# Three-layer graph convolution on one core: layer 1's edge gathers released by matmul units, weight loads moved, keys in bfloat16

## The chip, the cores and the metric

The kernel runs on one core of one Trainium2 chip. The core has five engines that run their own instruction streams and meet through semaphores: TensorE (PE, with its weight loads shown as PEld), VectorE (DVE), ScalarE (ACT), GpSimd (POOL) and SyncE (SP), which here only issues transfers. The metric is the device time of one execution in microseconds; lower is better.

## What is computed

A node table `x` of 2500 x 256 is normalized by rows and rectified. Then come three edge convolutions over 80,000 edges (`src`, `dst`, sorted by `dst`), and a final product over the input and the three layers' results.

```python
def _edge_conv(x, src, dst, W, b):
    xi = x[dst]
    xj = x[src]
    m = jnp.concatenate([xi, xj - xi], axis=-1) @ W + b
    s = jax.ops.segment_sum(m, dst, num_segments=N)
    cnt = jax.ops.segment_sum(jnp.ones((dst.shape[0],), m.dtype), dst, num_segments=N)
    return s / jnp.maximum(cnt, 1.0)[:, None]
...
h = jnp.maximum(_layernorm(x, axis=-1), 0.0)
xs = [h]
for W, b in ((W0, b0), (W1, b1), (W2, b2)):
    h = jax.nn.relu(_edge_conv(h, src, dst, W, b))
    xs.append(h)
return x + jnp.concatenate(xs, axis=-1) @ Wf + bf
```

Because the message is linear, a layer is `counts @ (h @ Wb)` plus a degree term times `h @ (Wt - Wb)`, where `counts` holds how often each source feeds each destination.

## The kernel before

**Tiling.** The 2500 nodes are padded to 20 tiles of 128 (`NT`). All but 112 of them (`FEW`) are destinations of 398 windows of 6 nodes. The windows form five groups (`NG`) of up to 80 windows, 480 destinations each. For a group the kernel holds `a`, the counts of 128 x 20 x 480. A count block is made of comparisons on VectorE (`compare`: one-hot `one_m`, `one_n` from the keys), small bfloat16 matmuls into a PSUM `bank` (`counts`) and casts by ScalarE (`take_counts`).

**Before layer 1.** The list `order` (line 1040) is written out by hand. Each name is a step: `st`, `rs`, `sq`, `sc` are row statistics, `N` normalizes a pair of tiles, `T` and `R` turn it on TensorE and take it into `hT` on ScalarE, `Z` and `F` are products, `H` and `L` split `Z` into a high part `zh` and a low part `zl`. `pick`, `pk`, `sg`, `se` find where each window's edges begin (`pick_half` on TensorE, `count_half` as a Sign pass on ScalarE, `search` on VectorE), `ge` fetches the edges with GpSimd, and `ka`, `km`, `kb`, `kt`, `k1`, `k2` make the keys: `key_low` and `key_high` write `km` and `kn` in float32, `key_turn` turns them by four transposes into a PSUM bank, `key_copy` spreads them. `warm8` and `warm12` put that many matmuls without use ahead of the next step that takes a bank (`keep_warm`, `warmed`). Every engine keeps the order in which the steps are written, since the calls go through `InOrder`.

**Layer 1.** The loop at line 1079 runs the five groups. `layer` (line 989) yields after each of 24 units: 20 units of four matmuls (two halves of the output, `zh` and `zl`), and four of `hT` by the weights `wt`. Between units the loop places pieces of other work: the building of the next group's counts (`build`), and a chain `extra` of smaller pieces, one piece a unit (up to two in group 0): `degrees(i)` counts the edges of each node with ScalarE passes and small matmuls, `finish` completes `a` and stores it to DRAM by SP for reuse in the later layers (four transfers of 1.2 MB), `later_loads` has SP load layer 2's weights `wb`, `wt`, `wf` and the bias rows `b_all`, `bf_sb`.

**The 112 few nodes.** They are summed edge by edge. `gather(0)` (line 918) issues 56 indirect transfers from GpSimd, each fetching one row of `z_dram` for each of 128 partitions, into the 8 slots of `sums` in turn; from the ninth on they add to the slot. They stand before the loop over the groups, and each waits only for the transfer eight before it. Their source `z_dram` is written by `keep_nodes`: `zh` by SP, `zl` added by GpSimd. After the last group `add_sums(8)` adds the eight slots by halving on VectorE and splits the result into two parts, and `layer_few` multiplies it in on TensorE. Layer 2 begins behind it.

Layers 2 and 3 have the same groups, with counts loaded back from DRAM and the few nodes' rows gathered in pairs (`gather_pairs`), every second gather of which waits for the unit that was issued last.

Of the kernel before, what the change touches and what calls it, by code (L numbers as in the profile page):

```python
# [8 lines left out]
F32 = mybir.dt.float32  # L9
I32 = mybir.dt.int32  # L10
AF = mybir.ActivationFunctionType
OP = mybir.AluOpType
# [256 lines left out]
BF16 = mybir.dt.bfloat16  # L269
# [19 lines left out]
def run(it):  # L289
    for _ in it:  # L290
        pass
# [16 lines left out]
def chain(*its):  # L308
    for it in its:
        yield from it  # L310
# [3 lines left out]
def by_windows(ctx: ExitStack, tc: tile.TileContext, x, src, dst, Ws, bs, Wf, bf, out, missing):  # L314
    nc = tc.nc
    PE, DVE, ACT, POOL, SP = nc.tensor, nc.vector, nc.scalar, nc.gpsimd, nc.sync
    PEo, DVEo, POOLo, ACTo, SPo = (InOrder(tc, e) for e in (PE, DVE, POOL, ACT, SP))
    P = 128
# [11 lines left out]
    CAP = CH * P  # L330
    SKIP = 2
    FEW = 112
    EDGES = 56
    SUMS = 8
# [3 lines left out]
    WG = (NW + P - 1) // P  # L338
# [3 lines left out]
    N1 = NT * (W - SKIP)  # L342
# [32 lines left out]
    def bank():  # L375
        return ps[-1].tile([P, 512], F32, name="bank")
# [16 lines left out]
    ident_b = const.tile([P, P], BF16, name="ident_b")  # L393
# [6 lines left out]
    lim = const.tile([P, WG], F32, name="lim")  # L400
# [3 lines left out]
    sums = const.tile([P, SUMS, D], F32, name="sums")  # L404
# [9 lines left out]
    pw = pre.enter_context(tc.tile_pool(name="prework", bufs=2))  # L414

    shift = pp.tile([P, P + 1], F32, name="shift")
    ident = shift[:, :P]
# [99 lines left out]
    first = pp.tile([P, 1], F32, name="first")  # L517
    after = pp.tile([P, 1], F32, name="after")
    behind = pp.tile([P, WG * P], F32, name="behind")
    pick = pp.tile([P, WG * P], F32R, name="pick")  # L520
# [104 lines left out]
        POOLo.tensor_scalar(who, who, NONE, None, op0=OP.add)  # L625

    def key_low(i):
        km = pw.tile([P, CAP], F32, name="km")
        ACTo.copy(km, parts[i][0])
        parts[i][0] = km  # L630

    def key_high(i):

        es = edges[i][0]
        hi_i = es if i < WG - 1 else pp.tile([P, CAP], I32, name="hi_i")
        DVEo.tensor_scalar(hi_i, es, ~(P - 1), 4, op0=OP.bitwise_and, op1=OP.logical_shift_right)
        kn = pw.tile([P, CAP], F32, name="kn")
        DVEo.scalar_tensor_tensor(kn, away[:, i, :], float(W + 1), hi_i, op0=OP.min, op1=OP.add)
        parts[i].append(kn)

    def key_turn(i):
        pt = bank()
        for q, k in enumerate(parts[i]):
            for j in range(CH):
                PEo.transpose(pt[:, q * CAP + j * P:q * CAP + (j + 1) * P], k[:, j * P:(j + 1) * P], ident)
        parts[i] = pt

    def key_copy(i, q):
# [229 lines left out]
    def finish(g, a):  # L878
        c0, n = group_of(g)
        if n < GS:  # L880
            DVEo.memset(a[:, :, n:].bitcast(F32), 0.0)
        ACTo.copy(a[PAD:PAD + 1, NT - 1, :n], cnt[PAD:PAD + 1, c0:c0 + n])
        if g + 1 < NG:
            store_a(g, a)
        yield
# [18 lines left out]
    def keep_nodes(l, a, b):  # L904
# [10 lines left out]
        for i, q in ways:  # L915
            POOLo.dma_start(to[:, i, q, :], tiles_of(zl)[:, i, q, :], accum_op=OP.add)

    def gather(l):

        for e in range(EDGES):  # L920
            POOLo.indirect_dma_start(
                out=sums[:, e % SUMS, :], out_offset=None, in_=z_dram[l][:, :],
                in_offset=bass.IndirectOffsetOnAxis(ap=who[:, e:e + 1], axis=0),
                **({"compute_op": OP.add} if e >= SUMS else {}))

    def add_sums(n):

        DVEo.scalar_tensor_tensor(sums[:, 0, :], b_all, deg[:, WG - 1, 0:1], sums[:, 0, :], op0=OP.mult, op1=OP.add)
        while n > 1:
            n //= 2  # L930
            DVEo.tensor_add(sums[:, :n, :], sums[:, :n, :], sums[:, n:2 * n, :])
        two = room(F32R)
        DVEo.tensor_copy(two[:, 0, :], sums[:, 0, :])
        DVEo.tensor_sub(two[:, 1, :], sums[:, 0, :], two[:, 0, :].bitcast(F32))
        return two
# [18 lines left out]
    def gather_pairs(l):  # L954

        got = []
        for k in range(EDGES // 2 + PAIRS):
            if k >= PAIRS:
                if k == PAIRS + 1:
                    DVEo.tensor_add(sums[:, :2, :], got[0], got[1])  # L960
                elif k > PAIRS:
                    DVEo.tensor_add(sums[:, :2, :], sums[:, :2, :], got[k - PAIRS])
            if k < EDGES // 2:
                two = room()
                got.append(two)
                for i in range(2):
                    d = POOLo.indirect_dma_start(
                        out=two[:, i, :], out_offset=None, in_=z_dram[l][:, :],
                        in_offset=bass.IndirectOffsetOnAxis(ap=who[:, 2 * k + i:2 * k + i + 1], axis=0))
                    if k >= PAIRS and i == 0:  # L970

                        tc.add_manual_dep(d.ins, unit[0].ins.name, mybir.DependencyInfo(
                            mybir.DependencyClass.Sync, mybir.DependencyReason.DATA), reason="spread over the layer")
            if k >= PAIRS - 1:
                yield

# [10 lines left out]
    unit = [None]  # L987

    def layer(l, g, a, own, PE=PE, ACT=ACT):
# [31 lines left out]
    a = new_a(0)  # L1021
# [16 lines left out]
        "warm": keep_warm,  # L1038
    }
    order = """  # L1040
        long warm8 lim io first next dstr st0 rs0 sq0 sc0 warm12 N0 pick pk00 sg00 pk01 sg01 st1 T0 pk11 R0 st4 rs1 sq1 pk30 se0
        sg11 sc1 Z0 pk20 N1 st5 sg30 ge0 T1 st6 R1 rs3 F0 sg20 pk21 sq3 st7 pk10 H0 F1 rs4 st3 sq4 sc4 G0 st9
        sc3 L0 sg21 N6 pk31 ka0 kb0 Z1 N5 st8 N7 G1 T6 rs5 sg10 sg31 km0 T5 se1 kt0 R6 H1 st2 F6 sq5 sc5 k10 k20
        rs2 Z6 ge1 L1 T7 B0 R5 R7 Z5 B1 C0 B2 ka1 G6 H6 N9 H5 C1 T9 F7 E0 ge2 kb1 R9 sq2 km1 E1 kt1 C2 B3 k21 Z9
        k11 N8 L6 B4 E2 L5 C3 B5 C4 T8 E3 E4 C5 V9 R8 E5 ge3 ka2 H9 sc2 Z7 H7 F8 G7 B6 N3 N2 ka3 km2 T2 R2 km3
# [19 lines left out]
    def later_loads():  # L1065
        load_wb(1, SPo)
        load_wt(1, SPo)
        load_wf(1, SPo)
        load_b_all(0, SPo)
        SPo.dma_start(bf_sb, bass.AP(tensor=bf.tensor, offset=bf.offset, ap=[[0, P], [1, D]]))  # L1070
        yield
# [2 lines left out]

    held = None
    LATE = [NT] * 4
    gather(0)
    extra = chain(degrees(0), finish(0, a), later_loads(), degrees(1))
    for g in range(NG):
        at = {}  # L1080
        own = LATE
        if g + 1 < NG:
            a1 = new_a(g + 1)
            one = build(g + 1, a1)
            left = -(-len([b for b in windows if b[0] == g + 1]) // TURN)
            units = NT + DC * DC
            at = {(i + 1) * (units - 1) // left - 1 for i in range(left)}
            if g:
                own = [u + 1 - i for i, u in enumerate(sorted(at)[1:5])]
        else:  # L1090
            extra = shares()
        for u, _ in enumerate(layer(0, g, a, own, PEo, ACTo)):
            if u in at:
                next(one)
            next(extra, None)
            if g == 0 and u % 2:
                next(extra, None)
            if g == 0 and u == NT // 2 + 3:
                by_count(0)
            if u == NT - 1 and g + 1 < NG:  # L1100
                run(extra)
                by_count(g + 1)
                if g == NG - 2:
                    by_count(NG)
        run(extra)
        if g + 1 < NG:
            run(finish(g + 1, a1))
            held, a = a, a1
        extra = chain(degrees(g + 2) if g + 2 < WG else ())
    layer_few(0, add_sums(SUMS))  # L1110
    DVEo.tensor_sub(ws[1][0], ws[1][0], ws[1][1])
    tiles = {NG - 1: a, NG - 2: held}
# [81 lines left out]
```

## Time and profile before

| | us |
|---|---|
| median of 3 runs | 502.18 (501.98 to 502.33) |
| the profiled execution | 508.13 |
| its span | 506.4 |
| end of the last vector instruction in it | 500.5 |
| start of layer 1's first group | 61.3 |
| start of layer 2's products | 205.3 |

The profile comes from an execution of its own, so its times add up to 508.13 and not to the median. Some stretches and groups to know (columns of the second block: line, engine, operation, out and in, count, busy time and mean, idle time before them):

```profile
DVE  7999987699898932581235141426722231214043
ACT  5676675563734330430000000005200000000000
POOL 3687307888888840005787582600175645451000
DMA  9426998696999991359798999973335889897033
```

Each digit is the busy share, in tenths, of one fortieth of the span (12.7 us). Layer 1 fills the fifth to the sixteenth digit.

```profile
L282 POOL DMA_INDIRECT sums<-z_dram,who x56 | 91.4, 1632 | 23.9 <-issue 16.8
L1004 PE MATMUL pa<-a,zh 128*128 128x480 f32 (+1 forms) x400 | 151.8, 380 | 0.0
L282 PE MATMUL bank<-one_n,one_m 128*128 128x120 bf16 (+1 forms) x796 | 43.2, 209 | 0.6 <-issue 0.4
```

The 56 gathers keep GpSimd busy for 1.63 us each. The main matmuls have a mean of 380 ns but overlap: in the chain of time 80 of them take 17.3 us, 0.217 us each. Instructions that go through `InOrder` all carry line 282, whatever step they come from.

### The profile page before, as it was taken

Reading aid. Unit: us, or ns where it says so; the run is one execution under the profiler, and the core shown is the slowest. Engines: PE = TensorE matmul, PEld = TensorE weight load, DVE = VectorE, ACT = ScalarE, POOL = GpSimd, SP = SyncE. Lnnn points to the kernel's source line nnn. Section 1 sums busy time; section 2 is a strip of 40 time slices with the busy share of each in tenths; the row PEclk is TensorE's granted clock in tenths of the full one; section 3 lists DMA queues with packets and bytes.
Section 4 is the critical chain, followed back from the end, with each engine's and each line's share of the span. In section 5 each row is a group of like instructions: output and inputs, shape, how many; then the busy total and the mean of one; then the engine's idle time right before and its main releaser. Section 6 shows DMA issues by size and latency. Waiting matters only on the chain.

```text
span 506.4 us, 7649 instructions
## 1 busy us (share of the span) xinstructions
PE 493.7 (97%) x2863; PEld 403.8 (80%) x2863; DVE 266.2 (53%) x670; ACT 136.2 (27%) x309; POOL 252.5 (50%) x234
## 2 busy tenths in 40 slices
PE   8999999899999999999999999999999999999994
PEld 4888887578888788888787878878887878788784
DVE  7999987699898932581235141426722231214043
ACT  5676675563734330430000000005200000000000
POOL 3687307888888840005787582600175645451000
PEclk9999999899999999999999999999999999999999
DMA  9426998696999991359798999973335889897033
GB/s 280 145 65 128 240 278 263 150 340 90 364 151 260 231 80 19 115 204 395 279 327 295 270 248 278 85 129 104 115 104 212 347 270 246 255 249 79 2 110 99
DMA packets 42104, 100.01 MB, mean 197 GB/s; under 512 B 5209, under 2 KB 32170, under 8 KB 36394
## 3 DMA queue, kind: packets, MB, share of 16 engines
q1 hardware_dynamic: 22762, 70.06, 37.6%
q0 software_dynamic: 18368, 28.26, 34.4%
q10 hardware_dynamic: 928, 1.11, 0.7%
q8 instruction: 24, 0.39, 0.3%
q14 instruction: 22, 0.18, 0.1%
HBM read 61.79 MB, written 38.26 MB: 198 GB/s over the span
## 4 chain that ended last, share of the span: by engine, by line
PE 91%; DVE 5%; DMA 1%; POOL 1%; issue 1%; ACT 0%; SPq 0%; DVEq 0%; ACTq 0%
PE pa L1004 34%; PE pa L282 22%; PE bank L811 10%; PE bank L282 8%; PE bank L787 7%; PE pa L1009 6%; PE pz L282 3%; DMA acc<-in_x_dram 1%; DVE st L282 1%; DVE one_m L282 1%; DVE one_n L282 1%; POOL acc L282 1%; DVE zl L282 0%; DVE mv L282 0%; DVE away L282 0%
## 5 line engine op out<-in xcount | busy, mean ns | idle before, releaser
L282 POOL DMA_INDIRECT one_m<-z_dram,who x112 | 113.0, 1009 | 151.1 <-DVE acc L282 79.7
L1004 PE MATMUL pa<-a,zh 128*128 128x480 f32 (+1 forms) x400 | 151.8, 380 | 0.0
L1004 PE MATMUL pa<-a,zl 128*128 128x480 f32 (+1 forms) x400 | 151.6, 379 | 0.0
L282 POOL DMA_INDIRECT sums<-z_dram,who x56 | 91.4, 1632 | 23.9 <-issue 16.8
L282 DVE TENSOR_TENSOR sums<-sums,one_m 128x512 f32<-128x512 f32 x52 | 36.0, 692 | 103.3 <-DMA one_m<-z_dram,who 101.2
L1004 PEld LDWEIGHTS pa<-a,zl 128*128 128x128 f32 x400 | 75.0, 187 | 12.0
L1004 PEld LDWEIGHTS pa<-a,zh 128*128 128x128 f32 x400 | 75.1, 188 | 10.4
L282 PE MATMUL pa<-a,zh 128*128 128x480 f32 (+1 forms) x200 | 81.2, 406 | 0.1
L282 DVE TENSOR_TENSOR one_m<-iota_m,key_m 128x1024 bf16<-128x1024 bf16 x100 | 68.8, 688 | 18.5 <-PE bank L282 15.4
L282 PE MATMUL pa<-a,zl 128*128 128x480 f32 (+1 forms) x200 | 75.7, 378 | 0.2 <-issue 0.2
L1012 ACT ACTIVATE hT<-pa 128x960 f32<-128x960 f32 (+1 forms) x10 | 9.7, 966 | 230.5 <-PE pa L1009 208.6
L282 ACT CAST a<-bank 128x480 fp32r<-128x480 f32 x100 | 51.7, 563 | 60.0 <-PE bank L282 52.7
L282 DVE TENSOR_TENSOR one_n<-iota_n,key_n 128x480 bf16<-128x480 bf16 x200 | 63.9, 360 | 0.0
L282 DVE SCALAR_TENSOR_TENSOR acc<-bank,share,acc 128x256 f32<-128x256 f32 x60 | 28.5, 483 | 58.7 <-PE bank L811 58.0
L811 PE MATMUL bank<-wf,hT 128*128 128x256 f32 x240 | 53.7, 379 | 0.5 <-ACT hT L282 0.5
L811 PEld LDWEIGHTS bank<-wf,hT 128*128 128x128 f32 x240 | 45.5, 190 | 9.8 <-issue 3.4
L282 PEld LDWEIGHTS <-one_m 128*128 128x128 bf16 x796 | 37.6, 98 | 10.5 <-issue 5.8
L282 PEld LDWEIGHTS pa<-a,zh 128*128 128x128 f32 x200 | 37.7, 188 | 8.8 <-issue 3.7
L282 PE MATMUL bank<-one_n,one_m 128*128 128x120 bf16 (+1 forms) x796 | 43.2, 209 | 0.6 <-issue 0.4
L282 PEld LDWEIGHTS pa<-a,zl 128*128 128x128 f32 x200 | 37.7, 188 | 6.9 <-issue 2.1
L787 PE MATMUL bank<-wb,hT 128*128 128x256 f32 x160 | 35.0, 380 | 0.0
L1009 PE MATMUL pa<-hT,wt 128*128 128x480 f32 (+1 forms) x80 | 33.8, 564 | 0.1
(148 smaller groups left out, 420.9 us busy)
## 6 DMA issues: line engine op xcount, KB each, us to landing
a<-a_dram SPq DMA_DIRECT2D x24, 1200.0 KB
a_dram<-a SPq DMA_DIRECT2D x20, 1200.0 KB
out_dram<-acc SPq DMA_DIRECT2D x19, 128.0 KB
z_dram<-one_m SPq DMA_DIRECT2D x16, 128.0 KB
z_dram<-sums SPq DMA_DIRECT2D x16, 128.0 KB
acc<-in_x_dram POOLq DMA_DIRECT2D x4, 512.0 KB
z_dram<-zh SPq DMA_DIRECT2D x7, 256.0 KB
z_dram<-zl POOLq DMA_DIRECT2D x7, 256.0 KB
```

Source lines behind the costliest of these rows:

```text
L282: return self.tc.keep_in_program_order(call(*args, **kwargs))
L787: PE.matmul(pz[:, :D], hT[:, c, t * P:(t + 1) * P], ws[l][1][:, c, :], start=(c == 0), stop=(c == DC - 1))
L811: PE.matmul(po[:, :D], hT[:, c, t * P:(t + 1) * P], wfs[l][:, c, :], start=(c == 0), stop=(c == DC - 1))
L1004: unit[0] = PE.matmul(pa[:, o, :n], tile_of(z, i)[:, o * P:(o + 1) * P], a[:, i, :n], start=(i == 0 and z is zh), stop=(z is zl and last[o ...
L1009: unit[0] = PE.matmul(pa[:, o, :n], ws[l][0][:, c, o * P:(o + 1) * P], hT[:, c, c0:c0 + n], start=False, stop=(last[o] == (kind, i, o)))
L1012: ACT.activation(hT[:, :, c0:c0 + n], pa[:, :, :n], AF.Relu)
```

## The change

Six edits stand in the diff:

- `km` and `kn` are bfloat16, and `key_turn` transposes them with the bfloat16 identity into a bank seen as bfloat16.
- In `order`, `N0 T0` come before `pick`, `R0` right after `pk00`, `Z0` before `pk11`; `warm12` becomes `warm8` and so stands ahead of `T0`.
- `gather` is a generator. The loop over the units takes a gather from it when enough units have passed: gather k from unit 10 + 1.4 k on for the first twelve, then one for every 1.2 units. Each gather gets a wait on the last matmul of the unit issued last (`behind_unit`).
- `later_loads` leaves the chain of group 0, where an empty step takes its place, and becomes the chain of group 3.
- `add_sums(8)` adds slots 4 to 6 to slots 0 to 2, then slots 1 to 3 to slot 0 one by one, and slot 7 last.
- `degrees` stays where it was.

```diff
     def key_low(i):
-        km = pw.tile([P, CAP], F32, name="km")
+        km = pw.tile([P, CAP], BF16, name="km")
...
-        kn = pw.tile([P, CAP], F32, name="kn")
+        kn = pw.tile([P, CAP], BF16, name="kn")
...
     def key_turn(i):
-        pt = bank()
+        pt = bank().bitcast(BF16)
         for q, k in enumerate(parts[i]):
             for j in range(CH):
-                PEo.transpose(pt[:, q * CAP + j * P:q * CAP + (j + 1) * P], k[:, j * P:(j + 1) * P], ident)
+                PEo.transpose(pt[:, q * CAP + j * P:q * CAP + (j + 1) * P], k[:, j * P:(j + 1) * P], ident_b)
         parts[i] = pt
...
+    def behind_unit(d):
+
+        tc.add_manual_dep(d.ins, unit[0].ins.name, mybir.DependencyInfo(
+            mybir.DependencyClass.Sync, mybir.DependencyReason.DATA), reason="spread over the layer")
+
     def gather(l):
 
         for e in range(EDGES):
-            POOLo.indirect_dma_start(
+            behind_unit(POOLo.indirect_dma_start(
                 out=sums[:, e % SUMS, :], out_offset=None, in_=z_dram[l][:, :],
                 in_offset=bass.IndirectOffsetOnAxis(ap=who[:, e:e + 1], axis=0),
-                **({"compute_op": OP.add} if e >= SUMS else {}))
+                **({"compute_op": OP.add} if e >= SUMS else {})))
+            yield
 
     def add_sums(n):
 
         DVEo.scalar_tensor_tensor(sums[:, 0, :], b_all, deg[:, WG - 1, 0:1], sums[:, 0, :], op0=OP.mult, op1=OP.add)
-        while n > 1:
-            n //= 2
-            DVEo.tensor_add(sums[:, :n, :], sums[:, :n, :], sums[:, n:2 * n, :])
+
+        if n > 2:
+            DVEo.tensor_add(sums[:, :3, :], sums[:, :3, :], sums[:, 4:7, :])
+            for i in (1, 2, 3):
+                DVEo.tensor_add(sums[:, 0, :], sums[:, 0, :], sums[:, i, :])
+        DVEo.tensor_add(sums[:, 0, :], sums[:, 0, :], sums[:, n - 1, :])
         two = room(F32R)
...
                     if k >= PAIRS and i == 0:
-
-                        tc.add_manual_dep(d.ins, unit[0].ins.name, mybir.DependencyInfo(
-                            mybir.DependencyClass.Sync, mybir.DependencyReason.DATA), reason="spread over the layer")
+                        behind_unit(d)
...
-        long warm8 lim io first next dstr st0 rs0 sq0 sc0 warm12 N0 pick pk00 sg00 pk01 sg01 st1 T0 pk11 R0 st4 rs1 sq1 pk30 se0
-        sg11 sc1 Z0 pk20 N1 st5 sg30 ge0 T1 st6 R1 rs3 F0 sg20 pk21 sq3 st7 pk10 H0 F1 rs4 st3 sq4 sc4 G0 st9
+        long warm8 lim io first next dstr st0 rs0 sq0 sc0 warm8 N0 T0 pick pk00 R0 sg00 pk01 sg01 st1 Z0 pk11 st4 rs1 sq1 pk30 se0
+        sg11 sc1 pk20 N1 st5 sg30 ge0 T1 st6 R1 rs3 F0 sg20 pk21 sq3 st7 pk10 H0 F1 rs4 st3 sq4 sc4 G0 st9
...
-    gather(0)
-    extra = chain(degrees(0), finish(0, a), later_loads(), degrees(1))
+    FIRST, SLOW = 10, 12
+    edge = gather(0)
+    fetched, passed = 0, 0
+    extra = chain(degrees(0), finish(0, a), [None], degrees(1))
...
         for u, _ in enumerate(layer(0, g, a, own, PEo, ACTo)):
+
+            passed += 1
+            while fetched < EDGES and passed >= FIRST + 1.4 * min(fetched, SLOW) + 1.2 * max(fetched - SLOW, 0):
+                next(edge)
+                fetched += 1
...
-        extra = chain(degrees(g + 2) if g + 2 < WG else ())
+        extra = chain(degrees(g + 2) if g + 2 < WG else later_loads() if g + 2 == WG else ())
     layer_few(0, add_sums(SUMS))
```

On the engines this gives: TensorE's transposes of the keys become pairs of a weight load and a matmul, GpSimd's instructions keep their order, SP has the five loads behind the twelve stores of groups 1 to 3 instead of ahead of them, and VectorE has one instruction more.

## The prediction

> **What bounds the kernel now.** I read the page first (busy shares, the chain that ended last), then the chain in order of time, then stretches of one layer-1 group each, then single engines where a stretch was too long.
>
> ```profile
> span 506.4 us, 7649 instructions
> PE 493.7 (97%) x2863; PEld 403.8 (80%) x2863; DVE 266.2 (53%) x670; ACT 136.2 (27%) x309; POOL 252.5 (50%) x234
> PE 91%; DVE 5%; DMA 1%; POOL 1%; issue 1%; ACT 0%; SPq 0%; DVEq 0%; ACTq 0%
> ```
>
> TensorE carries the time. In the chain by time VectorE leads from 8.65 to 34.75 us, GpSimd's normalizing takes 3.5 us, and from 38.30 us TensorE is on the chain almost without a break. Only work that TensorE does after 38.3 us, what starts it there, and gaps in it count. The gaps lie in one place, the end of group 0 of layer 1. Stretches of one group each (columns: busy time of PE, PEld, DVE, ACT, POOL, then granted clock, DMA share, GB/s):
>
> ```profile
> 61.30:84.45 23.15, 23.15 (x211) 19.63 (x209) 18.73 (x49) 15.80 (x46) 7.73 (x7) 1.00 0.93 278
> 84.45:91.14 6.69, 4.03 (x41) 2.57 (x41) 3.82 (x11) 2.75 (x8) 5.47 (x4) 1.00 0.58 155
> 91.14:97.21 6.07, 5.94 (x28) 2.73 (x26) 5.16 (x14) 2.84 (x7) 4.90 (x4) 0.72 0.46 65
> 97.21:125.48 28.27, 28.27 (x257) 22.98 (x258) 24.22 (x63) 15.67 (x39) 24.31 (x14) 1.00 0.88 241
> 125.48:154.09 28.61, 28.61 (x257) 23.05 (x256) 25.22 (x66) 16.20 (x41) 24.34 (x15) 1.00 1.00 235
> ```
>
> Groups 1 and 2 take 28.3 and 28.6 us; group 0 takes 35.9 (61.30 to 97.21). The chain there, and ScalarE just before:
>
> ```profile
> 84.61 0.73 PE bank L282 x16
> 85.34 0.11 issue
> ...
> 86.12 0.41 issue
> ...
> 88.97 0.48 issue
> ...
> 91.33 4.07 PE pa L282 x6
> ```
>
> ```profile
> 82.90 0.56 ACT L282 CAST a<-bank 128x480 fp32r<-128x480 f32 x1 [1.17 <-PE bank L282]
> 84.38 0.56 ACT L282 CAST a<-bank 128x480 fp32r<-128x480 f32 x1 [0.93 <-remote]
> 85.84 0.56 ACT L282 CAST a<-bank 128x480 fp32r<-128x480 f32 x1 [0.90 <-PE bank L282]
> ```
>
> "issue" means that TensorE waited for nothing the profile shows. Its count matmuls (bank) ended at 81.9 us, but the three casts that take them start 1.48 and 1.46 us apart, and TensorE's own instructions then come in clumps 0.7 us apart until 90.84. After that the clock is halved: six pa matmuls take 4.07 us. What the stretch should cost: 24 bank (1.07 us, as on the row at 100.05), 4 pa of 0.217, 12 degree matmuls (0.68, twice the part of six in the 1.41 row), 8 of hT by wt (3.22, the L1009 rows) and 16 bank (0.72): 6.56 us. It took 12.76. The stall is worth **6.2 us**.
>
> **What the Trainium skill says.** "TensorE: Matmul & The Clock Gate", Part 1, "What's actually happening": an idle window of about 3.4 us puts the array at half clock, a busy one restores it. The trace agrees: between 84.45 and 91.14 PE is busy 4.03 of 6.69 us, and the granted clock is 0.50 in 93 to 95 us. "Runtime: NRT & Kernel Launch", "Instruction fetch mechanics": instructions come over a DMA queue of their own in 16 KiB blocks. The trace has that queue (24 packets, 0.39 MB), one packet of it in 84 to 85 us, yet the clumps go on for five microseconds after it, so I do not rest the cause on it. The same page, "The ~15µs preamble/postamble breakdown", names a gap of about 6.2 us between a profile's total and the time of an execution without one. Here 508.13 - 502.18 = 5.95 us. I take this for the usual gap, that is, the stall is in the timed runs too; no run here shows it, and it is the largest doubt below.
>
> **The change part by part.**
>
> *Weights later.* Five loads leave SP's place at 76.03 to 79.99 us and go behind the stores of group 3, the last at about 157 us. In 76 to 85 us queue 1 moved 2.24 MB; 1.2 MB of that is a last store, 1.0 MB the loads, the last two of them 128 KB each in rows of 1 KB. They are the only thing in this stretch that no other group has: gathers run beside stores at 98 to 110 us, and alone at 112 to 125, with TensorE full. So I take the loads, in their mix with the first gathers, for the cause and credit the whole -6.2 us. Lower bound 0, if they are innocent or do the same at the new place; upper bound 6.5. What waits for them: wb at the L787 matmuls (205 us), b_all at the sums (185 us); landing near 170 us they are in time. SP carries nothing else between.
>
> *Gathers held back.* Gather k is released at unit 10 + 1.4k for the first twelve, then every 1.2 units. A unit is 28.4/24 = 1.19 us, in group 0 about 1.22 without the stall. Gather 0: unit 10 ends at 74.1 us, but it starts only at 76.36 anyway, behind the last zl add. Gather 5: unit 17, 82.1 us against 83.44 now; gather 9: unit 23, 89.5 against 89.54; gather 12: unit 27, 94.3 against 95.31. From there a release each 1.43 us meets a GpSimd that needs 1.54 + 0.30 = 1.85. So without the stall nothing moves by more than a microsecond. Behind the waiting gather GpSimd has only gathers. The wait itself: the layer-2 gathers with a TensorE wait already met show the same 0.30 us gap as those without. Cost 0; bound 0.03 us x 44 = 1.3 us at the end.
>
> *Last slot last.* Now:
>
> ```profile
> 182.96 1.54 POOL L282 DMA_INDIRECT sums<-z_dram,who  x1 [0.30 <-issue]
> 192.02 2.41 DVE L282 TENSOR_TENSOR sums<-sums 128x1024 f32<-128x1024 f32 x3 [5.98 <-DMA sums<-z_dram,who]
> 204.40 0.41 PE L282 MATMUL pa<-only,one_m 128*128 128x112 f32 x2
> ```
>
> The last gather lands at 192.0; adds (2.41) and split (0.72) end at 195.2; TensorE takes the result at 204.40: 9.2 us of cover. After the change one add (0.43) and the split follow the landing, 1.2 us. But the moved loads take 3.7 us of all DMA engines (queue 1 held 78.9% of them for the 9 us of 76 to 85, 7.1 us; a store of 1.2 MB at the 0.35 MB per us of group 3's stores is 3.4 of it), now inside 157 to 192 us, where the engines are full (share 1.00). The last landing goes to at most 195.7, the result is ready at 196.9, and TensorE, 6.2 us earlier, wants it at 198.2. Cover 1.3 us, cost 0; bound +2.4 if the landing slips by twice the loads' time.
>
> *bfloat16 keys.* Sixteen transposes. Four in float32 take 0.44 us (39.39 to 39.83); bf16 count matmuls of 100 columns on average take 1.07/24 = 0.045, so 128 columns 0.057 and four 0.23. Two of the four turns lie after 38.3 us: -0.42. The other two are behind VectorE: 0. The vector and scalar instructions that write the keys keep their number and shape: 0, bound -0.1 each.
>
> *First tiles ahead of the picks.* Eight warming matmuls instead of twelve, then TensorE turns tile pair 0 before the two pick matmuls; ScalarE takes hT (0.59) before the Sign passes; product Z0 (1.6 us) goes before pk11, pk30, pk20. Turn 0 can run at about 7.9 us (normalized at 7.81), the passes shift by 0.2. But pk11 waits behind Z0 until 10.8, its Sign pass slips from 10.67 to 11.2, and ScalarE's following normalizing and roots with it: VectorE's reciprocal at 15.18, which already waits 0.2 us for a root, comes 0.4 later, and VectorE's chain to 38.3 has no slack. +0.4; bounds 0 (ScalarE catches up in its 0.35 us pauses) and +0.8.
>
> *Degrees*: an empty step keeps their places: 0.
>
> Sum: -6.2 - 0.42 + 0.4 = -6.2. The profiled execution 508.13 becomes 501.9; less 5.95, the runs shown **496.0**.
>
> **The rivals.**
>
> *A, forecast, chance 0.47*: 496.0, own range 494.8 to 498.2 (early part -0.8, late sums +2.2).
>
> *B, nothing comes of it, 0.26*: the stall is only in profiled executions, stays with the gathers alone, or reappears near 165 us where the loads now mix with accumulating gathers. For it: the clumps last to 90.84, three microseconds after the last loads' packets, with gathers still going; and the 5.95 us gap is as large as the stall. Against: b_all's single load at 186 us beside gathers stalls nothing. What is left is -0.42 + 0.4: 502.2, from 501.2 to 503.2.
>
> *C, slower, 0.27*: the late sums become the bound at the end of layer 1. The place: layer_few's matmuls, with all of layer 2 queued behind them on TensorE. If the timed runs hold no stall, the cover is these 1.3 us and the landing slips by up to 7.4 us (loads in 1 KB rows taking turns with 1 KB gathers): 199.4 + 1.2 - 198.2 = +2.4 us, 504.6. It decides once the last landing passes 197.0 us (203.2 if the stall stays). For it: DMA share 1.00 from 125 to 184 us, a landing already 7.5 us behind the last issue. Against: with the stall gone the same slip only trims the gain.
>
> **How the numbers follow.** What this kernel's timing can tell from no change is about 0.2%, 1.0 us. Faster: A and 0.03 of B; same: 0.22 of B; slower: C with the rest of B, 0.28. The range, 494.8 to 504.0, holds A, B and a good part of C.
>
> **What would show it.** Right: in the new profile group 0 ends near 90.7 us, the clock stays at 1.00 in all of layer 1, no "issue" on the chain there; the five loads land near 165 to 170 us; the last gather lands by 196 and VectorE's sums never hold TensorE; the product chain starts within 0.5 us of 38.3. Wrong: clumps 0.7 us apart anywhere in 76 to 185 us, or a TensorE wait on VectorE's split before L787. If the profile loses 6 us and the timed runs do not, B's first reading holds.

## The result and the profile after

The changed kernel is slower: 505.39 us median of 8 executions (503.57 to 507.76), against 502.24 us (501.98 to 502.59) for the kernel before in the same comparison. The ratio is 1.0067, with a 95% interval of 1.0047 to 1.0086.

Executions of one and the same kernel differ here by 9 to 11 us on two of the three chips used below, so only times of one set, taken together on one chip, are compared, and a ratio leaves out the executions that lie more than 1.5% above the fastest of their kernel. The profile of the kernel before (508.13 us) shows an execution longer than any of its 8 timed ones in this comparison.

The profiled execution of the changed kernel took 505.69 us. Below are the head of its page and the shares of the chain that ended last:

```profile
span 504.0 us, 7694 instructions
PE 491.8 (98%) x2859; PEld 403.5 (80%) x2859; DVE 266.2 (53%) x672; ACT 135.1 (27%) x309; POOL 255.9 (51%) x234
PE 88%; DVE 4%; DMA 4%; issue 1%; POOL 1%; ACT 1%; SPq 0%; DVEq 0%; ACTq 0%
```

TensorE's share of the chain fell from 91 to 88% and that of transfers rose from 1 to 4%: something that was hidden now lies on the path. The stretches say where (columns: start and end, length, busy time of PE, PEld, DVE, ACT and POOL, granted clock, DMA share, GB/s):

```profile
61.79:90.98 29.19, 29.19 (x273) 24.00 (x272) 25.56 (x68) 20.07 (x57) 11.91 (x11) 1.00 0.70 215
90.98:119.33 28.35, 28.35 (x246) 22.39 (x246) 25.07 (x66) 16.07 (x40) 24.69 (x13) 1.00 0.82 230
178.69:203.69 25.00, 22.41 (x119) 18.62 (x119) 5.18 (x14) 1.65 (x3) 9.90 (x7) 0.97 0.82 70
198.50:207.00 8.50, 5.91 (x24) 4.94 (x23) 4.66 (x10) 2.21 (x4) 0.00 (x0) 0.80 0.10 31
```

Group 0 is clean: TensorE is busy through all of it. The loss is at the end of layer 1, where it is idle for 2.6 us and then runs below full clock. The chain there, in order of time:

```profile
187.03 11.36 DMA sums<-z_dram,who
...
198.51 0.97 DVE sums L282
...
201.67 0.44 DVE one_m L282
...
202.15 1.74 PE pa L282 x7
203.89 18.18 PE bank L787 x80
```

It starts with a gather on GpSimd, the last but one, which lands 11.4 us after its issue, and goes through VectorE's five additions to TensorE. The instructions, engine by engine (start, duration, engine, line, operation, out and in, and in brackets the idle time before and what ended it):

```profile
89.74 5.34 POOL L282 DMA_INDIRECT sums<-z_dram,who  x1 [1.30 <-PE pa L282]
...
102.34 1.53 POOL L282 DMA_INDIRECT sums<-z_dram,who  x1 [0.30 <-PE pa L282]
...
188.87 1.54 POOL L282 DMA_INDIRECT sums<-z_dram,who  x1 [0.30 <-issue]
...
198.51 2.80 DVE L282 TENSOR_TENSOR sums<-sums 128x768 f32<-128x768 f32 x5 [9.10 <-DMA sums<-z_dram,who]
...
201.69 0.92 PE L282 MATMUL pa<-only,one_m 128*128 128x112 f32 x2 [2.45 <-DVE one_m L282]
```

The first three of these are the ninth, the thirteenth and the last gather. The ninth, released at 89.74 us by a unit of TensorE, keeps GpSimd for 5.34 us instead of some 1.6. The thirteenth is issued at 102.34 us (95.31 before), the last at 188.87 (182.96 before), and TensorE waits 2.45 us for the sums.

### The profile page after: what moved, and what is told of

It reads as the page before. It is cut to its first block, busy times and chain, and to the rows that moved or that the text cites. A ratio compares the mean times of both kernels' runs of the same rounds, so it can differ in the third digit from the quotient of the medians.

```text
span 504.0 us, 7694 instructions
## 1 busy us (share of the span) xinstructions
PE 491.8 (98%) x2859; PEld 403.5 (80%) x2859; DVE 266.2 (53%) x672; ACT 135.1 (27%) x309; POOL 255.9 (51%) x234
## 4 chain that ended last, share of the span: by engine, by line
PE 88%; DVE 4%; DMA 4%; issue 1%; POOL 1%; ACT 1%; SPq 0%; DVEq 0%; ACTq 0%
PE pa L1011 34%; PE pa L282 19%; PE bank L811 10%; PE bank L282 7%; PE bank L787 7%; PE pa L1016 6%; PE pz L282 4%; DMA sums<-z_dram,who 2%; DMA wb<-in_L_gnn_W_dram 1%; DVE one_m L282 1%; DVE one_n L282 1%; POOL acc L282 1%; DVE sums L282 1%; DVE zl L282 0%; DVE st L282 0%
## 5 line engine op out<-in xcount | busy, mean ns | idle before, releaser
L282 POOL DMA_INDIRECT sums<-z_dram,who x56 | 95.5, 1706 | 26.8 <-PE pa L282 14.3
L282 DVE TENSOR_TENSOR one_m<-iota_m,key_m 128x1024 bf16<-128x1024 bf16 x100 | 69.0, 690 | 13.3 <-PE bank L282 12.3
L282 ACT CAST a<-bank 128x480 fp32r<-128x480 f32 x100 | 50.6, 566 | 55.2 <-PE bank L282 54.3
L787 PEld LDWEIGHTS bank<-wb,hT 128*128 128x128 f32 x160 | 30.9, 195 | 4.3
## 6 DMA issues: line engine op xcount, KB each, us to landing
a_dram<-a SPq DMA_DIRECT2D x20, 1200.0 KB, 11.4
```

The costliest lines, as they stand in the source:

```text
L282: return self.tc.keep_in_program_order(call(*args, **kwargs))
L787: PE.matmul(pz[:, :D], hT[:, c, t * P:(t + 1) * P], ws[l][1][:, c, :], start=(c == 0), stop=(c == DC - 1))
```

## The experiments

**First set: the parts alone, on one chip.** The kernel before stood there at 509.81 us median (503.57 to 514.16, 59 executions).

*The kernel before, one execution* (no edit).

> The kernel before, unchanged, for a second profile. Theory 1 (the stall at 85 to 96 us belongs to single executions and not to the kernel): a span of about 500.4 us, layer 1's group 0 in 29 us instead of 35.9, no clumps, granted clock 0.999; the sums of the few nodes ready at 195 us, about 3 us ahead of TensorE's need at 198. Rival (the stall is in every execution): a span near 506, group 0 again 35 us.

Measured: 512.87 us, span 511.1, with clumps of TensorE work in group 0. The chain there:

```profile
85.67 0.25 PE bank L282 x2
85.92 0.47 issue
...
87.09 0.35 PE bank L282 x4
87.44 1.09 issue
```

The stall of the profile before is back: two or four matmuls, then half a microsecond in which nothing that the profile shows holds TensorE. The landing of the sums (195.52 us) plays no part, because TensorE is late itself and takes them at 208.02.

*The hold alone.*

```
-            POOLo.indirect_dma_start(
+            behind_unit(POOLo.indirect_dma_start(
...
+            while fetched < EDGES and passed >= FIRST + 1.4 * min(fetched, SLOW) + 1.2 * max(fetched - SLOW, 0):
+                next(edge)
+                fetched += 1
```

> Before with the gathers released by units and nothing else. Theory H (holding the gathers back makes the last landing late): the last gather is issued about 5 us later than in the kernel before, the sums end after TensorE needs them, +1 to +4 us. Theory W (the weights' new place is what delays the landing): issue of the last gather within 1 us of before, time within 0.5 us of 502.2.

Measured: 505.53 us (503.52 to 509.25), ratio 0.9930 (0.9900 to 0.9960). Group 0 has no stall although the loads are in their old place. In the profile the fourth gather keeps GpSimd for 5.50 us, the last is issued at 188.07, and TensorE waits 2.17 us.

*The late loads alone.*

```
-    extra = chain(degrees(0), finish(0, a), later_loads(), degrees(1))
+    extra = chain(degrees(0), finish(0, a), [None], degrees(1))
-        extra = chain(degrees(g + 2) if g + 2 < WG else ())
+        extra = chain(degrees(g + 2) if g + 2 < WG else later_loads() if g + 2 == WG else ())
```

> Before with the five loads behind the stores of group 3 and nothing else. Theory W: the last landing 3.7 us or more later, the sums late by 1 to 4 us, 503 to 506 us. Theory H: within 0.5 us of 502.2. If the loads beside the first gathers cost anything in undisturbed executions, it would be below 502.

Measured: 506.37 us (501.87 to 511.19), ratio 0.9961 (0.9926 to 0.9995). The profiled execution, 501.87 us, is the fastest of the 22. It has no such stall (TensorE idles 0.4 us in all from 61.5 to 92 us) and no wait for the sums; others of the same kernel reach 511 us and were not profiled.

*Keys and first tiles alone* (float32 `km` and `kn` to bfloat16, and the first two lines of `order`).

> Before with bfloat16 keys and the first tiles ahead of the picks, nothing else. By the prediction's steps -0.42 and +0.4: within 0.3 us of 502.2, the first long chain of products on TensorE starting 0.4 us later than at 38.3 us and the two late key turns 0.2 us shorter each. Rival (the reorder costs nothing that lasts): 501.8.

Measured: 510.73 us (503.56 to 512.47), ratio 1.0002 (0.9958 to 1.0045), with the stall. So each of the hold and the late loads seems to make the stall rarer, while nothing of the kind is seen from the early parts.

**Second set, on the same chip**, the kernel before at 508.96 us (503.71 to 514.46, 58 executions).

*The changed kernel.*

> The changed kernel itself, beside the kernel before on the same chip. Theory (POOL's chain): once the 13th gather is issued, POOL needs 86 to 88 us for the other 44 (1.54 us each and 0.30 between them), so a gather that is issued late is never caught up; expected here the 13th at about 102 us, the last issue at 189, the sums' landing at 198 to 199, TensorE waiting 2 to 3 us for one_m at the end of layer 1, 505 to 506 us. If the kernel before stands at 508 to 510 on this chip because of its stall at 85 to 95 us, the change reads as faster here (ratio 0.990 to 0.993) although it was slower where the kernel before had no stall. Rival (the late loads' packets delay the landing): the 13th gather may come earlier, and landing is over 12 us after the last issue.

Measured: 503.06 us (501.34 to 510.17), ratio 0.9878 (0.9818 to 0.9939), thus faster than the kernel before here. Five of 8 executions are at 503.3 or below, three at 508.5 or above; the profiled one, 510.17 us, has the long ninth gather (5.49 us), its last gather at 189.53 and a wait of 4.0 us.

*All but the hold* (the edit of the hold taken out of the changed kernel again).

> The change without the release by units: gathers are issued as POOL gets to them. Theory: the 13th gather at 96 to 97, the last at 183 to 185 us, no wait of TensorE for one_m of over 0.5 us, undisturbed executions at 502 to 502.6; 2.5 to 3.5 us below the changed kernel where neither stalls; some executions stall, as the run with the weights later alone had them. Rival (late loads): the wait stays at 1 us or more and the time at 504 or more in every execution. If the hold is what keeps the stall away, the median is above that of the changed kernel on a chip that stalls.

Measured: 506.31 us (501.63 to 510.23), ratio 0.9932 (0.9899 to 0.9964). Its profile, at 507.50 us, stalls in group 0 (12.68 us busy of 14.98) and does not wait for the sums. So late loads without the hold do not always keep the stall away.

*All but the new order of additions.*

```
-        if n > 2:
-            DVEo.tensor_add(sums[:, :3, :], sums[:, :3, :], sums[:, 4:7, :])
...
+        while n > 1:
+            n //= 2
+            DVEo.tensor_add(sums[:, :n, :], sums[:, :n, :], sums[:, n:2 * n, :])
```

> The change with the old order of the sums' additions. Theory: all slots land together at the end, so the new order, 2.80 us after the landing, is 0.4 us longer than the old one's 2.41, and this kernel is 0.4 us faster than the changed kernel. The prediction's step: the last slot lands 1 us or more after the others, and the old order is 1 to 2 us slower.

Measured: 507.84 us (501.76 to 510.36), ratio 0.9973 (0.9937 to 1.0010). The times spread too far to tell 0.4 us; inconclusive. Its profile (503.23 us) shows the hold without a long gather: the ninth takes 1.66 us, the thirteenth is at 97.75, the last at 186.48, and the wait is 0.71 us.

*A faster release.*

```
-            while fetched < EDGES and passed >= FIRST + 1.4 * min(fetched, SLOW) + 1.2 * max(fetched - SLOW, 0):
+            while fetched < EDGES and passed >= FIRST + 1.1 * min(fetched, SLOW) + 1.2 * max(fetched - SLOW, 0):
```

> The changed kernel with 1.1 units a gather instead of 1.4 for the first twelve (12 x 0.3 x 1.19 = 4.3 us earlier at the 13th). Theory: the 13th gather at 96 to 99, the last issue at 183 to 186, TensorE's wait for one_m under 0.5 us, undisturbed executions 502 to 503, so 2 to 3 us below the changed kernel. Rival (it is the long issue of one gather of the first twelve, 5.3 us, that costs the time, whatever the release): the 13th at 100 or later, and no more than 1 us gained.

Measured: 505.42 us (502.80 to 509.42), ratio 0.9966 (0.9937 to 0.9995). In the profile the thirteenth gather is at 98.53, the last at 185.54, the wait 0.47 us, as the theory had it; but the gain of 2 to 3 us over the changed kernel did not come, the median being 2.4 us above that kernel's.

**Third set, on another chip, where the kernel before does not stall**: 502.51 us (502.06 to 503.61, 43 executions).

*The kernel before as a kernel of its own* (no edit).

> The kernel before, as a kernel of its own, so that another execution of it is seen with a profile. Theory (the stall at 85 to 95 us is no part of the program but comes in some executions): the times fall into groups, about 502 to 505 us without it and 508 to 513 us with it; an execution profiled at under 505 us shows TensorE busy through 76 to 91 us, the 13th gather at 95 to 96 us and the sums' result before TensorE wants it. Rival (the stall is in every execution, as the prediction's sum had it): TensorE is idle for 2 us or more in 76 to 91 us in this profile too, whatever its time.

Measured: 502.33 us (502.08 to 503.53), ratio 0.9999 (0.9991 to 1.0007). This is what the prediction had lacked, a profile of an undisturbed execution (502.47 us, span 500.6); only the thirteenth gather comes at 100.11 us instead of the expected 95 to 96. Its stretch of group 0, same columns as above:

```profile
61.79:90.98 29.19, 29.19 (x272) 23.95 (x271) 25.55 (x68) 20.26 (x58) 12.86 (x11) 1.00 0.83 250
```

and its timeline of the gathers, the sums and TensorE's use of them:

```profile
90.59 4.27 POOL L282 DMA_INDIRECT sums<-z_dram,who  x1 [0.30 <-issue]
...
100.11 1.74 POOL L282 DMA_INDIRECT sums<-z_dram,who  x1 [0.30 <-issue]
...
184.74 1.54 POOL L282 DMA_INDIRECT sums<-z_dram,who  x1 [0.30 <-issue]
...
195.53 2.41 DVE L282 TENSOR_TENSOR sums<-sums 128x1024 f32<-128x1024 f32 x3 [10.82 <-DMA sums<-z_dram,who]
...
198.30 0.43 DVE L282 TENSOR_TENSOR one_m<-sums,one_m 128x256 fp32r<-128x256 f32 x1
...
198.79 0.41 PE L282 MATMUL pa<-only,one_m 128*128 128x112 f32 x2
```

VectorE ends the split at 198.73 and TensorE takes it at 198.79. The kernel before, undisturbed, has next to no cover at the end of layer 1: 0.06 us by the end of the split, about 0.5 for the first product, which needs only the first of the two parts (ready at 198.26). In the profile before TensorE was 6 us late, and the same place seemed to have 9.2 us.

*All but the late loads* (the loads back in their place).

> The change with layer 2's loads in their old place (issued at 76 to 80 us). Theory: the hold alone keeps TensorE from stalling in group 0, and POOL's chain alone makes the sums late: TensorE busy through 76 to 91 us, times like the changed kernel's, 501.5 to 503 us when the 13th gather is issued by 98 us and 505 to 510 when one of the first twelve is held up for 5 us. The prediction's step (moving the loads takes the stall away): TensorE stalls here as in the kernel before. Rival (the late loads delay the landing): landing within 9 us of the last issue and 1 us or more faster than the changed kernel.

Measured: 502.97 us (500.80 to 505.09), ratio 1.0017 (1.0001 to 1.0032). No stall in group 0; the ninth gather takes 5.33 us, the last is issued at 188.60 and lands by 197.55, 8.95 us later; the wait is 1.53 us. A landing within 9 us is what the rival about the late loads asked for; in the changed kernel's first profile it is 9.64 us. The changed kernel was not run on this chip, so the times of the two cannot be compared.

*A slower release* (2.6 units a gather in place of 1.4).

> The changed kernel with 2.6 units a gather for the first twelve instead of 1.4. Theory (POOL's chain): the 13th gather at 110 to 111 us, 86 to 88 us later the last issue, at 197 to 198, landing 9.5 to 10 us after it, TensorE's wait for one_m 10 to 12 us and then some 1 us at half clock: 511 to 515 us. Rival (gathers catch up, since later ones land faster): the last issue before 193 us and under 508 us.

Measured: 514.50 us (514.01 to 514.66), ratio 1.0239 (1.0224 to 1.0254). The timeline of the thirteenth and last gather, the sums and TensorE:

```profile
114.02 2.28 POOL L282 DMA_INDIRECT sums<-z_dram,who  x1 [2.12 <-PE pa L282]
...
197.74 1.54 POOL L282 DMA_INDIRECT sums<-z_dram,who  x1 [0.30 <-issue]
...
206.81 2.80 DVE L282 TENSOR_TENSOR sums<-sums 128x768 f32<-128x768 f32 x5 [9.45 <-DMA sums<-z_dram,who]
...
209.99 0.92 PE L282 MATMUL pa<-only,one_m 128*128 128x112 f32 x2 [10.89 <-DVE one_m L282]
```

The last issue, the landing, the wait and the time are where the theory put them, though by two misses that cancel: the thirteenth gather came 3 us later than it said, and only 83.7 us passed from it to the last instead of 86 to 88. This is the clearest test: a gather released late is paid for at the end of layer 1.

*A mixture*: the faster release, late loads and bfloat16 keys, with the old additions and the old first tiles.

> A mixture meant to be better than both: the gathers released at 1.1 units each for the first twelve, the loads late, bfloat16 keys, but the old order of the sums' additions and the first tiles where they were before. Theory: the end of layer 1 shows no wait of TensorE over 0.3 us (the old order gives 0.4 us back), the chain starts 0.4 us earlier, undisturbed executions at 501 to 502 us and no stall in group 0; median 1 us or more below that of the release at 1.1 units alone. Rival: other waits take their place and the times are the same as there.

Measured: 503.57 us (500.69 to 508.01), ratio 1.0026 (1.0006 to 1.0047). A miss: the profiled execution has a gather of 4.27 us at 90.57, its last at 187.75, and a wait of 2.83 us. The mixture is not ahead of the kernel before on this chip.

**Fourth set, on a third chip**, because the parts had been seen alone only where the kernel before mostly stalled. The kernel before: 502.89 us (502.30 to 511.06, 67 executions), 40 of them at 502.3 to 503.2 and 27 at 505.1 or above.

*Hold alone.*

> The hold alone, again, beside the changed kernel, the late loads alone and the change without the hold on one chip. In an undisturbed execution of the kernel before the sums' result comes 0.06 us before TensorE wants it, so every microsecond by which the sums are late is paid. If the hold is the part that costs, this kernel has a wait of 1.5 us or more for one_m in its profile and stands at 1.5 to 3 us over the kernel before, the late loads alone at 0 to 0.5 us. If the late loads are the part, it is the other way round. If each adds, both stand at about 1 us and the changed kernel at their sum.

*Late loads alone.*

> The late loads alone, again. Where the kernel before runs without its stall: 0 to 0.5 us over it if the hold is the part that costs (landing at 195.5 to 196, no wait over 0.3 us); 1.5 us or more over it, with landing 12 us or more after the last issue, if the late loads' packets are.

*All but the hold.*

> The change without the hold, again. Where the kernel before runs without its stall: as fast as it, plus 0.3 us of the earlier parts and up to 0.4 us of the longer last additions (502.3 to 503), if the hold is the part that costs; 1.5 us or more over it, if late loads and late additions are.

*The changed kernel.*

> The changed kernel again, as the measure for the three. Where the kernel before runs without its stall: 505 to 506 us, 3 us over it; a wait of 2 to 4 us for one_m. Where the kernel before stalls in part of its executions: below its median.

| | median us | lowest to highest | over 505.5, of 20 | ratio |
|---|---|---|---|---|
| late loads alone | 502.10 | 501.13 to 505.81 | 2 | 0.9964 (0.9934 to 0.9994) |
| all but the hold | 503.82 | 500.84 to 508.49 | 8 | 0.9989 (0.9954 to 1.0025) |
| hold alone | 504.15 | 502.14 to 507.56 | 7 | 0.9985 (0.9950 to 1.0020) |
| the changed kernel | 507.29 | 501.60 to 510.58 | 12 | 0.9993 (0.9954 to 1.0032) |

The ratios take in most of the stalled executions of the kernel before (25 of its 67 lie above 505.5 us); that is why a kernel can have the higher median and a ratio below 1. Only the interval of the late loads lies wholly below 1. Beside the 40 undisturbed executions of the kernel before (median 502.7), the medians lie 0.6 us lower for the late loads, 1.1 higher for all but the hold, 1.5 for the hold alone and 4.6 for the changed kernel. These sizes are rough: they set all executions of one kernel against chosen ones of another, and all of these kernels but the hold alone end sooner after their last vector instruction than the kernel before, by some 1.6 us (see "The sum that came out").

Of what was expected, the hold's 1.5 to 3 us are just met, though its profile, of a good execution, shows no wait; all but the hold lies 0.8 us above the 503 named as its upper end and the changed kernel 1.3 above its 506.

The late loads alone are the best version found: ahead of the kernel before in both sets in which they ran (0.9961 and 0.9964), and with 2 of 20 executions above 505.5 us where the changed kernel has 12. On the chip where the kernel before does not stall they were not run, and there their lead is not shown.

The profile of the hold alone was of a good execution (502.54 us), and its gathers show what is different in one:

```profile
89.26 1.64 POOL L282 DMA_INDIRECT sums<-z_dram,who  x1 [1.06 <-PE pa L282]
...
182.61 1.54 POOL L282 DMA_INDIRECT sums<-z_dram,who  x1 [0.31 <-PE pa L282]
```

The ninth gather, held by a unit as in the changed kernel, takes 1.64 us, and the sums are not late. The changed kernel's second profile (508.04 us) has it at 5.33 us again:

```profile
89.92 5.33 POOL L282 DMA_INDIRECT sums<-z_dram,who  x1 [1.06 <-PE pa L282]
```

All profiles with the hold, put side by side (rows in the order of the thirteenth gather; times in us):

| profile | longest issue of the first 12 | 13th gather | last gather | TensorE waits |
|---|---|---|---|---|
| hold alone, fourth set | 1.66 | 96.96 | 182.61 | 0 |
| old additions | 1.66 | 97.75 | 186.48 | 0.71 |
| faster release | 2.58 | 98.53 | 185.54 | 0.47 |
| mixture | 4.27 | 99.54 | 187.75 | 2.83 |
| hold alone, first set | 5.50 | 101.81 | 188.07 | 2.17 |
| all but late loads | 5.33 | 102.33 | 188.60 | 1.53 |
| changed kernel, three profiles | 5.33 to 5.49 | 102.34 to 102.53 | 188.76 to 189.53 | 2.45 to 4.04 |
| slower release | 5.50 | 114.02 | 197.74 | 10.89 |

The pace of the release matters less than the one long issue: at 1.4 units a gather the thirteenth comes at 97.0 and 97.8 us where no issue is long and at 101.8 to 102.5 where one takes over 5 us, and at 1.1 units with one of 4.27 us (the mixture) at 99.5. Of the four profiles without the hold and without the stall, one has a long gather (4.27 us, the undisturbed kernel before), and one waits for the sums, for 0.3 us (all but the hold, fourth set).

## Why the prediction was wrong

The forecast, faster by 6 us, failed. What happened is rival C at its place, the late sums, together with the first reading of rival B, that the stall was not in the timed executions.

*The stall taken for part of every execution: the step that failed.* The prediction read the 5.95 us between the profile and the median as "the usual gap, that is, the stall is in the timed runs too", resting on "Runtime: NRT & Kernel Launch", "The ~15µs preamble/postamble breakdown" of the Trainium skill, which names about 6.2 us between a profile's total time and the reported time of an execution. But 508.13 and 502.18 are both reported times of executions, and the gap between a profile and its own execution is another one: the time around the span is 1.7 us in the profile before (508.13 - 506.4), 1.7 in the changed kernel's and 1.9 in the undisturbed profile of the kernel before (502.47 - 500.6). The 5.95 us were the stall itself (506.4 - 500.6 = 5.8). In the comparison that counted no execution of the kernel before had it (501.98 to 502.59 us), so there was nothing to win.

*Late loads take the stall away: half right.* In the 14 profiles with the hold, the late loads or both one stalls (all but the hold, second set); of the four profiles with neither, three do. On the chip of the first two sets alone it is one of six against two of two. So the direction held, but the same is had from the hold with the loads in their old place (no stall in its two profiles, nor in the one without late loads), and the undisturbed kernel before has loads and gathers mixed and does not stall. Loads mixed with the first gathers are thus not the cause by themselves, as the step had it. The transfer of instructions that the prediction set aside does not tell the cases apart either: it falls between 84 and 87 us in three stalled profiles and in three that do not stall, and at 82 in the fourth stalled one. What stalls TensorE is open.

*Gathers held back, cost 0: failed in its size.* By the step's rule the ninth gather falls to unit 22, about 88.3 us; it was released at 89.74, so the releases ran over a microsecond late. Above all, the step took GpSimd's time for one gather as fixed. One of the first twelve was held up for 4.3 to 5.5 us in seven of ten profiles with the hold, against one of eight without it. From the thirteenth on GpSimd has only gathers, most of them 1.54 us each and 0.30 between, and from the issue of the thirteenth to that of the last pass 83.7 to 89.3 us in all profiles: most of a delay is not caught up. In the changed kernel's profile the thirteenth is 2.2 us later and the last 4.1 us later than in the undisturbed kernel before. The other 1.9 us come after the thirteenth, nearly all from gathers that take longer (73.16 us for 43 of them instead of 71.52); no run tells why.

*Last slot last, cover 1.3 us: failed.* It took the landing at 192.0 us from the one execution it had. In the undisturbed one the sums land at 195.53 and in the stalled one of the first set at 195.52, so that the kernel before, undisturbed, has a cover of 0.06 us where the step's figures give 3.0 (198.2 - 195.2). In the changed kernel the sums land at 198.5 instead of 195.7 at most, the split ends 3.6 us behind that instead of 1.2, and TensorE wants it at 199.24 instead of 198.2: the cover of 1.3 us became a lack of 2.9. Nor did the new order give time back: the path went through the last but one gather (issued at 187.03, landed 11.4 us later), whose additions take 2.80 us instead of 2.41. The term "one add and the split, 1.2 us" holds only for the last slot.

*Late loads delay the landing.* The delay is smaller than the bound of 3.7 us: from the last issue to the sums' first addition without the hold it is 9.1 to 10.8 us in four profiles with early loads and 11.4 to 12.3 in four with late ones, 1.4 us in the mean. The loads themselves land late, at 178.8 to 182.2 us for the third and the fifth in the changed kernel, not near 165 to 170. They can hold up the issue as well. In the late loads alone, fourth set, GpSimd waits for the transfer eight before:

```profile
170.14 1.75 POOL L282 DMA_INDIRECT sums<-z_dram,who  x1 [0.77 <-DMA sums<-z_dram,who]
...
176.09 1.54 POOL L282 DMA_INDIRECT sums<-z_dram,who  x1 [1.92 <-DMA sums<-z_dram,who]
```

Beyond the usual 0.30 us such waits come to 0.3 to 2.4 us in six of the eleven profiles with late loads, and to nothing in the seven with early ones. Rival C had the direction right, but the hold is the larger part: with the loads back in their place the last gather was still issued at 188.60 and the sums landed at 197.55, against 188.87 and 198.51 with late loads. That the 504.6 us of rival C lie near the measured 505.39 is luck, since it put the slip down to the loads alone.

*The early parts: right in size, but not kept.* First two lines from the chain of the undisturbed kernel before, then two from that of the changed kernel:

```profile
39.87 0.44 PE bank L282 x4
...
42.03 0.82 PE bank L282 x12
...
40.04 0.22 PE bank L282 x4
...
42.05 0.58 PE bank L282 x12
```

The turn of the keys went from 0.44 to 0.22 us and the second from 0.82 (turn and counts) to 0.58: -0.46, forecast -0.42. (The transposes were pairs of a weight load and a matmul before the change too; what is new is their type.) The product chain begins at 38.66 to 39.11 us in the ten profiles with the new first tiles, against 38.25 to 38.79 in the eight with the old ones: 0.3 us later in the mean, forecast 0.4. But at the start of layer 1 nothing of the gain is left:

```profile
61.60 0.57 PE L282 MATMUL pa<-a,zh 128*128 128x480 f32 x1
...
61.79 0.56 PE L282 MATMUL pa<-a,zh 128*128 128x480 f32 x1
```

The first line is of the undisturbed kernel before, the second of the changed kernel. In the mean of the profiles layer 1 starts at 61.80 us with the new first tiles and at 61.49 with the old ones, still 0.3 us later. Part of the gain goes at 47.6 us, where 16 count matmuls take 1.15 us instead of 0.87.

*The sum that came out.* From the undisturbed kernel before to the changed kernel, by their profiles (500.6 to 504.0 us): TensorE reaches the few nodes 0.45 us later, waits 2.45, takes 2.20 instead of 1.08 us for the few nodes' own products (which wait once more for the second part, and run in part at half clock), and the products behind them take 18.18 instead of 17.33 us. Together that is 4.87 us, and it is still there at the last vector instruction, 4.84 us later (first the undisturbed kernel before, then the changed kernel):

```profile
494.13 0.48 DVE acc L282
...
498.97 0.48 DVE acc L282
```

The span grew by only 3.4 us, because it ends 4.5 us behind that instruction instead of 6.0. The prediction has no term for this. It goes with the program and not with the chip: 5.9 to 6.1 us in the profiles of the kernel before, of the early parts alone and of the hold alone, 4.3 to 4.6 in all others, those of the late loads alone (4.3) and of all but the late loads (4.5) among them. What makes it shorter is open. The medians differ by 3.15 us.

## What to carry to other kernels

Before a stall in a profile is priced, compare the profiled execution's time with the timed ones: if they differ by as much as the stall, the stall may be in that execution alone. The cover of a hidden chain must be read from an undisturbed execution too, since a stall on the bounding engine lends every other chain its length: here 9.2 us of cover in the stalled profile were 0.06 in the undisturbed one. A chain of transfers issued nearly back to back by one engine to the end of a stage had no reserve here: where the first ones were delayed, the last ones were. And when two programs are compared, read the time at the last useful instruction as well as the whole: 1.4 us of the loss were hidden behind it.

## What the runs showed of the hardware

The issue of one gather on GpSimd is not a constant: 0.94 to 1.5 us for most of the first eight, 1.53 and more from the ninth on (these add to their slot), some of them 2 to 3.7, and now and then one of 4.3 to 5.5. All nine that took over 4 us end a fixed time after VectorE has finished a run of comparisons (`one_m`, `one_n`), 0.82 to 0.83 us for those among the first eight and 1.42 to 1.45 for those that add, though that moment lies anywhere from 85.6 to 94.0 us. So it is in the changed kernel, whose ninth gather ends at 95.08:

```profile
92.98 0.65 DVE L282 TENSOR_TENSOR one_n<-iota_n,key_n 128x480 bf16<-128x480 bf16 x2
95.03 0.69 DVE L282 TENSOR_TENSOR one_m<-iota_m,key_m 128x1024 bf16<-128x1024 bf16 x1 [1.40 <-PE bank L282]
```

VectorE is idle from 93.63 us on, and the gather ends 1.45 us later, about what it takes in other executions. "DMA: Bandwidth & Descriptors", "SWDGE vs HWDGE vs iDMA" of the Trainium skill says that GpSimd writes such a transfer's descriptors into on-chip memory and can be locked out of it by VectorE in one of VectorE's modes; the long issues fit that. It is not shown as their cause: no run changed VectorE's work there or tells whether these comparisons use that mode, other gathers run beside the same comparisons in 1.1 us, and in the hold alone, fourth set, the ninth starts at the same place of VectorE's work (0.21 us into `one_n`) and takes 1.64 us.

Waits of 2.17, 2.45, 2.99 and 4.04 us were followed by half clock: behind them the 80 matmuls of the next product took 18.15, 18.18, 19.01 and 19.62 us instead of 17.33, yet behind one of 2.83 us 17.33. "TensorE: Matmul & The Clock Gate", Part 1, "What's actually happening", of the Trainium skill names an idle window of about 3.4 us and that it runs free of the work, which would allow such a spread; three of these waits are shorter than the figure.
